# The last 64 rows of a down projection, multiplied in the row halves of TensorE's array, in groups of eight between two output tiles

## The chip, the core and the metric

The kernel runs on one core of one Trainium2 chip. The metric is the device time of one execution in microseconds (us). It was 488.84 us as the median of three runs (487.09, 488.84 and 489.75).

## What is computed

The reference applies a low-rank adapter that is selected for each batch entry, feeds its output through a gated feed-forward block with FP8-quantized activations and weights, and adds the result to the input. Cut to what matters:

```python
x: (8, 256, 1024)                      # 2048 tokens of H = 1024
Bx  = einsum('bni,bri->bnr', x,  B[ids])        # rank 16
c   = einsum('bnr,bor->bno', Bx, A[ids])
gate = q8(c) @ gate_w.T ;  up = q8(c) @ up_w.T  # I = 2752 columns each
hidden = silu(gate) * up
out = x + q8(hidden) @ down_w.T                 # contraction over I = 2752
```

`q8` clips and rounds to FP8 and multiplies the scale back in. The change is in the last product. Its contraction length is 2752 = 21 x 128 + 64, so that one chunk of 64 rows is left over.

## The kernel before

All activations lie transposed, features on the 128 partitions and tokens along the free dimension. The 2048 tokens are cut into four blocks of 512 (`NTB = 4`, `TB = 512`). The contraction and output dimension H is cut into eight tiles of 128 (`NH = 8`), the inner dimension I into 22 chunks (`NI = 22`), of which the last has 64 rows (`TAIL = 64`). TensorE takes 128 x 128 weights, of which `high` picks the upper 16 bits (bf16) out of the 32-bit words that lie in memory, and streams 512 columns of FP8 activations past them.

The program has three stages.

1. *Adapter*, the first 47 us. Products with the small matrices B and A give the FP8 activations `xg`. The products with A (`times_a` at L456, `four_times_a` at L491) have a contraction of only 16; each goes into one of four row groups of the array (partitions 0, 32, 64 and 96 onwards), and the four of a round write four different PSUM tiles `c0` to `c3`. They stand in the middle of full-array products of the next stage: for instance `gate_up(2, 0, between=...)` at L562 puts 32 of them between the gate products and the up products of a block.
2. *Gate and up* (`gate_up`, L503 to L543). For each chunk c of I and each token block t, eight products for the gate and eight for the up values; ScalarE takes the silu (L525) and VectorE multiplies it with the up values into `hid[c]` in FP8 (L526). For the last chunk, gate and up share one set of weights of 64 + 64 columns, so there are eight products. Its gate values come out on PSUM partitions 0 to 63, its up values on 64 to 127, and its result is written to partitions 64 to 127 of `hid[21]`. The partitions 0 to 63 of `hid[21]`, and those of the tail's weight tile `wt`, are set to zero by GpSimd at the start (L393, L394).
3. *Down* (L594 to L623). For each output tile k of 8 and each block t of 4, 22 products run into one PSUM tile `yd`: 21 with the full chunks, and one with `wt` and `hid[21]`, whose upper 64 rows carry the tail and whose lower 64 are the zeros. VectorE scales the sum and adds the residual x (L618), and the result goes out by a DMA on SP's queue (L621).

The order of work on TensorE is the program order of these loops. PSUM is one pool of eight one-bank tiles in rotation (tag `ps`). Weights come through a pool of five 1 MB tiles (`wpool`): each k of Down takes two of them, and their loads (L599) stand in SP's queue together with the output DMAs. ScalarE reads every weight tile and every activation tile once for a check of the values (`note_low_bits` L403, `note_squares` L410). The check's count is read near the end (`outside`, L575), and a general version of the kernel runs instead if the count isn't zero, which with these inputs it is. The tail's weights `wt` come by one DMA (L571), issued at 27.5 us.

Of the kernel before, what the change touches and what calls it, by code (L numbers as in the profile page):

```python
# [8 lines left out]
F32 = mybir.dt.float32  # L9
BF16 = mybir.dt.bfloat16  # L10
FP8 = mybir.dt.float8e4
# [3 lines left out]
ALU = mybir.AluOpType  # L15
AX = mybir.AxisListType

P = 128
T = 2048
# [6 lines left out]
NI = (I + P - 1) // P  # L26
TAIL = I - (NI - 1) * P
TB = 512
NTB = T // TB
# [14 lines left out]
def high(ap):  # L44

    return ap.bitcast(BF16)[..., 1::2]


def low(ap):
    return ap.bitcast(U16)[..., 0::2]  # L50
# [201 lines left out]
def adaln_ffn(  # L252
# [13 lines left out]
    nc = tc.nc  # L266
    const = ctx.enter_context(tc.tile_pool(name="const", bufs=1))
    psum = ctx.enter_context(
        tc.tile_pool(name="psum", bufs=8, space=bass.MemoryType.PSUM)
    )  # L270
# [10 lines left out]
    NSQ = 2 * NTB + NI  # L281
# [5 lines left out]
    with ExitStack() as fast:  # L287
        acts = fast.enter_context(tc.tile_pool(name="acts", bufs=1))
        lora = fast.enter_context(tc.tile_pool(name="lora", bufs=1))
        wpool = fast.enter_context(tc.tile_pool(name="w", bufs=5))  # L290
        work = fast.enter_context(tc.tile_pool(name="work", bufs=3))


        xs = [acts.tile([P, NH, TB], F32, name=f"x{t}") for t in range(NTB)]
        xg = [acts.tile([P, NH, TB], FP8, name=f"xg{t}") for t in range(NTB)]
        hid = [acts.tile([P, T], FP8, name=f"hid{c}") for c in range(NI)]

# [41 lines left out]
        def load_gate_up(c):  # L341
            n = NH if c == NI - 1 else 2 * NH
            w = wpool.tile([P, 2 * NH, P], F32, tag="w", name="w_gu")[:, :n]
            at = c * 2 * NH * P
            nc.sync.dma_start(  # L345
                out=w, in_=w_gu[:, at : at + n * P].rearrange("p (k n) -> p k n", n=P)
            )
            w_of[c] = w
# [30 lines left out]
        down_s = const.tile([P, 1], F32, name="down_s")  # L379
# [10 lines left out]


        wt = acts.tile([P, NH, P], F32, name="w_dt")
        nc.gpsimd.memset(wt[:TAIL], 0.0)  # L393
        nc.gpsimd.memset(hid[NI - 1][:TAIL], 0.0)  # L394

        def junk_like(ap):
            size = prod(ap.shape[1:])
            junk = work.tile([P, 2 * NH * P], BF16, tag="junk", name="junk", bufs=1)
            return shaped(junk[:, :size], ap)

        def note_low_bits(w, rows, column):
            tc.keep_in_program_order(
                nc.scalar.activation(  # L403
                    junk_like(w), low(w), AF.Copy, accum_out=lows[:rows, column : column + 1]
                )
            )

        def note_squares(q, rows, column):
            tc.keep_in_program_order(
                nc.scalar.activation(  # L410
                    junk_like(q), q, AF.Square, accum_out=squares[:rows, column : column + 1]
                )
            )
# [28 lines left out]
        def round_to(to, c, engine):  # L442
            scale = inv[:, GATE_IN : GATE_IN + 1]
            if engine is nc.vector:
                nc.vector.tensor_scalar(to, c, scale, None, ALU.mult, saturate=False)  # L445
            else:
                nc.scalar.activation(to, c, AF.Copy, scale=scale, saturate=False)  # L447
# [37 lines left out]
        def four_times_a(bm, pairs):  # L485
            for i in pairs:
# [11 lines left out]
                for q in range(4):  # L498
                    to = xg[2 + q // 2][:, 2 * i : 2 * i + 2, bass.ts(q % 2, SEQ)]
                    round_to(to, cs[q], nc.vector if q % 2 else nc.scalar)  # L500


        def gate_up(c, t, between=None):  # L503
            tail = c == NI - 1
            w = w_of[c]
            cols = bass.ts(t, TB)
            ys = []
            for j in range(1 if tail else 2):
                y = psum.tile([P, TB], F32, tag="ps", name=f"y{j}")
                order = ORDER if t < 2 else range(NH)  # L510
                for k in order:
                    nc.tensor.matmul(  # L512
                        y,
                        lhsT=high(w[:, j * NH + k, :]),
                        rhs=xg[t][:, k, :],
                        start=(k == order[0]),
                        stop=(k == order[-1]),
                    )
                ys.append(y)
                if between and not j:  # L520
                    between()
            gates, ups = (ys[0], ys[-1]) if not tail else (ys[0][:TAIL], ys[0][TAIL:])
            rows = slice(TAIL, P) if tail else slice(0, P)
            g = work.tile([P, TB], F32, tag="g", name="g")
            nc.scalar.activation(g[rows], gates, AF.Silu, scale=gate_s[: gates.shape[0]])  # L525
            nc.vector.scalar_tensor_tensor(  # L526
                hid[c][rows, cols],
                in0=ups,
                scalar=up_by_down[rows],
                in1=g[rows],  # L530
                op0=ALU.mult,
                op1=ALU.mult,
                saturate=False,
            )
            if c > 1 and t == (NTB - 1 if c == 2 else 1):
                for done in {2: (0, 2), 3: (1, 3)}.get(c, (c,)):
                    note_low_bits(w_of[done], P, done)
                if c <= 1 + 2 * NTB:
                    i, half = divmod(c - 2, 2)
                    ks = slice(half * NH // 2, (half + 1) * NH // 2)  # L540
                    note_squares(xg[i][:, ks, :], P, c - 2)
                for done in (0, 1) if c == 2 else (c - 1,):
                    note_squares(hid[done], P, 2 * NTB + done)  # L543
# [13 lines left out]
        bm = times_b(1, b_pad)  # L557
# [3 lines left out]
        bm = four_times_b()  # L561
# [6 lines left out]
        for c in range(3, NI):  # L568
            load_gate_up(c)
            if c == NI - 2:  # L570
                nc.sync.dma_start(out=wt[TAIL:], in_=w_d_tail)  # L571
            for t in range(NTB):
                gate_up(c, t)

        def outside():  # L575

            nc.vector.tensor_scalar(ok[:, :NLOW], lows, 0.0, None, ALU.is_le)
            nc.vector.tensor_scalar(
                ok[:, NLOW : NLOW + NSQ], squares, SAME_MAX**2, None, ALU.is_lt
            )  # L580
            least = const.tile([P, 1], F32, name="least")
            nc.vector.tensor_reduce(least, ok, AX.X, ALU.min)
            found = const.tile([P, 1], F32, name="found")
            nc.vector.tensor_scalar(found, least, 0.5, None, ALU.is_lt)
            ones = const.tile([P, 1], F32, name="ones")
            nc.vector.memset(ones, 1.0)
            count = psum.tile([P, TB], F32, tag="ps", name="count")
            nc.tensor.matmul(count[:1, :1], lhsT=found, rhs=ones, start=True, stop=True)  # L588
            count_i = const.tile([1, 1], I32, name="count_i")
            nc.vector.tensor_copy(count_i, count[:1, :1])  # L590
            return nc.values_load(count_i[0:1, 0:1], min_val=0, max_val=P)


        for k in range(NH):  # L594
            ws = []
            for half in range(2):
                n = HALF - half
                w = wpool.tile([P, 2 * NH, P], F32, tag="w", name="w_d")[:, :n]
                nc.sync.dma_start(out=w, in_=w_d[k][:, half * HALF : half * HALF + n, :])  # L599
                note_low_bits(w, P, NI + 2 * k + half)  # L600
                ws += [w[:, i, :] for i in range(n)]
            if k == 0:
                note_squares(hid[NI - 1], P, NSQ - 1)
                note_low_bits(wt, P, NLOW - 1)
            for t in range(NTB):
                cols = bass.ts(t, TB)
                y = psum.tile([P, TB], F32, tag="ps", name="yd")
                for c in range(NI):
                    tail = c == NI - 1
                    nc.tensor.matmul(  # L610
                        y,
                        lhsT=high(wt[:, k, :] if tail else ws[c]),
                        rhs=hid[c][:, cols],
                        start=(c == 0),
                        stop=tail,
                    )
                o = work.tile([P, TB], F32, tag="o", name="o")
                nc.vector.scalar_tensor_tensor(  # L618
                    o, in0=y, scalar=down_s, in1=xs[t][:, k, :], op0=ALU.mult, op1=ALU.add
                )  # L620
                nc.sync.dma_start(out=outT[bass.ts(k, P), cols], in_=o)  # L621
                if k == NH - 1 and t == NTB - 2:
                    others = outside()  # L623

    with tc.If(others > 0):
        general(
# [78 lines left out]
```

## Time and profile before

| | |
|---|---|
| median of three runs | 488.84 us (487.09 to 489.75) |
| the profiled execution | 486.88 us, of which the profile's span is 485.1 us |
| granted TensorE clock | 0.996 |
| TensorE (PE) busy | 476.7 us, 98% of the span |
| VectorE (DVE) busy | 105.1 us, 22% |
| ScalarE (ACT) busy | 192.0 us, 40% |
| GpSimd (POOL) busy | 2.9 us, 1% |
| gate and up products (L512) | 298.2 us busy in 1376 |
| down products, full chunks (L610 with `w_d`) | 150.3 us busy in 672 |
| down products, tail (L610 with `w_dt`) | 12.1 us busy in 32 |
| DMA | 52.39 MB, mean 108 GB/s |

Matmuls are pipelined, so the duration of one (379 ns) overlaps that of the next. The distance from one start to the next is what a product costs in a row of them. A line of the timeline gives the start in us, the length in us, the engine, the source line, the operation with its tiles and shapes, and how many instructions are merged in it. In brackets stands the engine's idle time before it, with what ended it. PEld is the loading of weights, which overlaps PE. `SPq` is SP's queue, which issues DMAs.

### The profile page before, as it was taken

The numbers are of one execution on the slowest core, as the hardware profiler recorded it, in microseconds if no ns is written. First come the engines' busy times: TensorE is split into PE (matmuls) and PEld (weight loads), VectorE is DVE, ScalarE is ACT, GpSimd is POOL, SyncE is SP. The second block draws the span as 40 slices with busy tenths as digits, with TensorE's granted clock in tenths as the row PEclk, the third lists the DMA queues.
The fourth block names the chain that finished last, engine by engine and source line by source line (L and its number), as shares of the span: only waits on it lengthen the run. The fifth ranks groups of instructions, "written<-read, shape, count | busy, mean of one in ns | idle before, by whom it ended". The sixth has DMA issues, their size and how long they took to land.

```text
span 485.1 us, 5786 instructions
## 1 busy us (share of the span) xinstructions
PE 476.7 (98%) x2416; PEld 224.2 (46%) x2416; DVE 105.1 (22%) x159; ACT 192.0 (40%) x243; POOL 2.9 (1%) x6
## 2 busy tenths in 40 slices
PE   8999999999999999999999999999999999999995
PEld 8445444444444444444444444444444444444442
DVE  1435221212121212121212121222111111112111
ACT  1234239955556654534354545459102112011000
POOL 2000000000000000000000000000000000000000
PEclk9999999999999999999999999999999999999998
DMA  8996004422221112222221011113514515423111
GB/s 297 331 388 245 1 0 176 172 86 88 86 88 56 42 77 88 86 86 88 86 65 36 31 59 55 61 55 104 157 69 154 168 62 171 120 103 120 43 67 50
DMA packets 13092, 52.39 MB, mean 108 GB/s; under 512 B 1538, under 2 KB 2562, under 8 KB 9474
## 3 DMA queue, kind: packets, MB, share of 16 engines
q1 hardware_dynamic: 12768, 51.80, 30.9%
q8 instruction: 21, 0.34, 0.3%
q10 hardware_dynamic: 290, 0.14, 0.1%
q14 instruction: 13, 0.11, 0.1%
HBM read 43.55 MB, written 8.39 MB: 107 GB/s over the span
## 4 chain that ended last, share of the span: by engine, by line
PE 91%; DMA 6%; SPq 2%; issue 0%; DVE 0%
PE y L512 58%; PE yd L610 31%; DMA w_gu<-w_gu 5%; PE c L491 1%; SPq L337 1%; SPq L319 0%; SPq L312 0%; DMA ids_i<-ids 0%; SPq L317 0%; DVE o L618 0%; SPq L345 0%; SPq L331 0%; PE count L588 0%
## 5 line engine op out<-in xcount | busy, mean ns | idle before, releaser
L512 PE MATMUL y<-xg,w_gu 128*128 128x512 fp8e4 x1376 | 298.2, 379 | 0.8 <-ACT xg L447 0.5
L512 PEld LDWEIGHTS <-w_gu 128*128 128x128 bf16 x1376 | 134.2, 98 | 164.1 <-issue 2.2
L610 PE MATMUL yd<-hid,w_d 128*128 128x512 fp8e4 x672 | 150.3, 379 | 0.0
L525 ACT ACTIVATE g<-y,gate_s 128x512 f32<-128x512 f32 (+1 forms) x88 | 60.0, 683 | 146.8 <-PE y L512 146.7
L526 DVE SCALAR_TENSOR_TENSOR hid<-y,up_by_down,g 128x512 fp8e4<-128x512 f32 (+1 forms) x88 | 66.0, 751 | 225.7 <-PE y L512 158.3
L610 PEld LDWEIGHTS <-w_d 128*128 128x128 bf16 x672 | 65.7, 98 | 79.1
L403 ACT ACTIVATE junk<-w_d 128x1408 bf16<-128x1408 uint16 (+1 forms) x16 | 21.2, 1324 | 89.2 <-DMA w_d<-w_d 89.1
L618 DVE SCALAR_TENSOR_TENSOR o<-yd,down_s,x 128x512 f32<-128x512 f32 x32 | 24.0, 750 | 122.0 <-PE yd L610 122.0
L410 ACT ACTIVATE junk<-hid 128x2048 bf16<-128x2048 fp8e4 x22 | 41.9, 1906 | 0.5
L403 ACT ACTIVATE junk<-w_gu 128x2048 bf16<-128x2048 uint16 (+1 forms) x22 | 41.0, 1865 | 0.1
L410 ACT ACTIVATE junk<-xg 128x2048 bf16<-128x2048 fp8e4 x8 | 15.3, 1906 | 0.2
L447 ACT ACTIVATE xg<-c,inv 128x512 fp8e4<-128x512 f32 x16 | 9.7, 688 | 13.8 <-PE c L456 12.1
L445 DVE TENSOR_SCALAR xg<-c,inv 128x512 fp8e4<-128x512 f32 x16 | 10.9, 744 | 6.8 <-PE c L456 3.8
L610 PE MATMUL yd<-hid,w_dt 128*128 128x512 fp8e4 x32 | 12.1, 379 | 0.0
L550 PE MATMUL warm<-zeros 128*128 128x128 bf16 x78 | 7.4, 287 | 1.0 <-DVE zeros L277 1.0
L431 PE MATMUL bx<-x,b_pad 128*64 128x256 f32 x64 | 7.7, 382 | 0.3 <-DVE b_pad L420 0.3
L550 PEld LDWEIGHTS <-zeros 128*128 128x128 bf16 x78 | 7.2, 136 | 1.0 <-DVE zeros L277 1.0
L431 PEld LDWEIGHTS bx<-x,b_pad 128*64 128x64 f32 x64 | 5.5, 137 | 2.1 <-DVE b_pad L420 0.5
L610 PEld LDWEIGHTS <-w_dt 128*128 128x128 bf16 x32 | 3.1, 98 | 3.8
L456 PE MATMUL c<-bm,a_sel 16*128 16x256 f32 x64 | 4.0, 387 | 0.5 <-DVE bm L439 0.5
L403 ACT ACTIVATION_READ_ACCUMULATOR junk<-w_gu 128x1 f32 x22 | 4.2, 192 | 0.0
L410 ACT ACTIVATION_READ_ACCUMULATOR junk<-hid 128x1 f32 x22 | 4.1, 188 | 0.0
(37 smaller groups left out, 31.5 us busy)
## 6 DMA issues: line engine op xcount, KB each, us to landing
w_gu<-w_gu SPq DMA_DIRECT2D x21, 1024.0 KB, 4.9
outT<-o SPq DMA_DIRECT2D x32, 256.0 KB, 2.1
x<-x SPq DMA_DIRECT2D x7, 1024.0 KB, 8.9
w_d<-w_d SPq DMA_DIRECT2D x8, 704.0 KB, 5.0
w_d<-w_d SPq DMA_DIRECT2D x8, 640.0 KB, 3.8
x<-x SPq DMA_DIRECT2D x2, 512.0 KB, 5.8
a_sel<-a SPq DMA_DIRECT2D x4, 128.0 KB, 5.5
w_gu<-w_gu SPq DMA_DIRECT2D x1, 512.0 KB
```

Source lines behind the costliest of these rows:

```text
L337: nc.sync.dma_start(out=xs[t][:, ks, :], in_=x4[t][:, ks, :])
L403: nc.scalar.activation(junk_like(w), low(w), AF.Copy, accum_out=lows[:rows, column : column + 1])
L410: nc.scalar.activation(junk_like(q), q, AF.Square, accum_out=squares[:rows, column : column + 1])
L431: nc.tensor.matmul(bx[64 * j : 64 * (j + 1)], lhsT=b_pad[:, j, k].rearrange("p o r -> p (o r)"), rhs=xs[t][:, k, bass.ts(j, SEQ)], start=( ...
L445: nc.vector.tensor_scalar(to, c, scale, None, ALU.mult, saturate=False)
L447: nc.scalar.activation(to, c, AF.Copy, scale=scale, saturate=False)
L512: nc.tensor.matmul(y, lhsT=high(w[:, j * NH + k, :]), rhs=xg[t][:, k, :], start=(k == order[0]), stop=(k == order[-1]),)
L525: nc.scalar.activation(g[rows], gates, AF.Silu, scale=gate_s[: gates.shape[0]])
L526: nc.vector.scalar_tensor_tensor(hid[c][rows, cols], in0=ups, scalar=up_by_down[rows], in1=g[rows], op0=ALU.mult, op1=ALU.mult, saturate=F ...
L550: nc.tensor.matmul(warm[:, :P], lhsT=zeros, rhs=zeros, start=(i == 0), stop=(i == 77))
L610: nc.tensor.matmul(y, lhsT=high(wt[:, k, :] if tail else ws[c]), rhs=hid[c][:, cols], start=(c == 0), stop=tail,)
L618: nc.vector.scalar_tensor_tensor(o, in0=y, scalar=down_s, in1=xs[t][:, k, :], op0=ALU.mult, op1=ALU.add)
```

## The change

- The tail's hidden values get a tile of their own, `hid_tail`, of bf16 with 128 partitions, 2 and 512. Odd blocks lie on partitions 0 to 63, even blocks on partitions 64 to 127 (`half_of`), two blocks along the free dimension. VectorE first writes the FP8 values into a small tile `tail`, and then copies them to `hid_tail` as bf16.
- The tail's weights are loaded twice, into both partition halves of `wt`. The zeros, and GpSimd's two memsets that wrote them, are gone.
- In Down the tail's products have 64 rows, and two blocks lie in the two row halves of the array (`tail_of`). They are grouped: after the 4 x 21 full products of an even k come the four tail products of this k, and at once the four tail products of k + 1, which open the PSUM tiles of k + 1. Then follow the 4 x 21 full products of k + 1, of which the last closes each tile.
- For an even k the four evictions (`finish`) come together behind its tail group. For an odd k each follows its block, as before.
- `note_squares` for the tail reads `hid_tail`, 1024 elements of a partition instead of 2048.

```diff
-        hid = [acts.tile([P, T], FP8, name=f"hid{c}") for c in range(NI)]
+        hid = [acts.tile([P, T], FP8, name=f"hid{c}") for c in range(NI - 1)]
+        hid_tail = acts.tile([P, 2, TB], BF16, name="hid_tail")
...
-        nc.gpsimd.memset(wt[:TAIL], 0.0)
-        nc.gpsimd.memset(hid[NI - 1][:TAIL], 0.0)
...
+        def half_of(t):
+            return slice(0, TAIL) if t % 2 else slice(TAIL, P)
...
+            if tail:
+                to = lora.tile([P, 2 * TB], FP8, tag="bm", name="tail", bufs=2)[half_of(t), :TB]
+            else:
+                to = hid[c][:, cols]
...
             nc.vector.scalar_tensor_tensor(
-                hid[c][rows, cols],
+                to,
...
+            if tail:
+                nc.vector.tensor_copy(hid_tail[half_of(t), t // 2], to)
...
-                nc.sync.dma_start(out=wt[TAIL:], in_=w_d_tail)
+                for t in range(2):
+                    nc.sync.dma_start(out=wt[half_of(t)], in_=w_d_tail)
...
+        def tail_of(k, ys, start):
+            for t in range(NTB):
+                nc.tensor.matmul(
+                    ys[t],
+                    lhsT=high(wt[half_of(t), k, :]),
+                    rhs=hid_tail[half_of(t), t // 2],
+                    start=start,
+                    stop=not start,
+                )
+
+        def finish(k, t, y):
+            o = work.tile([P, TB], F32, tag="o", name="o")
+            nc.vector.scalar_tensor_tensor(
+                o, in0=y, scalar=down_s, in1=xs[t][:, k, :], op0=ALU.mult, op1=ALU.add
+            )
+            nc.sync.dma_start(out=outT[bass.ts(k, P), bass.ts(t, TB)], in_=o)
...
-                note_squares(hid[NI - 1], P, NSQ - 1)
+                note_squares(hid_tail, P, NSQ - 1)
...
+            first = k % 2 == 0
+            if first:
+                ys = [psum.tile([P, TB], F32, tag="ps", name=f"yd{t}") for t in range(NTB)]
             for t in range(NTB):
-                cols = bass.ts(t, TB)
-                y = psum.tile([P, TB], F32, tag="ps", name="yd")
-                for c in range(NI):
-                    tail = c == NI - 1
+                for c in range(NI - 1):
                     nc.tensor.matmul(
-                        y,
-                        lhsT=high(wt[:, k, :] if tail else ws[c]),
-                        rhs=hid[c][:, cols],
-                        start=(c == 0),
-                        stop=tail,
+                        ys[t],
+                        lhsT=high(ws[c]),
+                        rhs=hid[c][:, bass.ts(t, TB)],
+                        start=(first and c == 0),
+                        stop=(not first and c == NI - 2),
                     )
...
+                if not first:
+                    finish(k, t, ys[t])
                 if k == NH - 1 and t == NTB - 2:
                     others = outside()
+            if first:
+                tail_of(k, ys, start=False)
+                for t in range(NTB):
+                    finish(k, t, ys[t])
+                ys = [psum.tile([P, TB], F32, tag="ps", name=f"yd{t}") for t in range(NTB)]
+                tail_of(k + 1, ys, start=True)
```

More of the change, by code (lines that the diff above doesn't have):

```diff
@@ L602, in adaln_ffn @@
             if k == 0:
-                note_squares(hid[NI - 1], P, NSQ - 1)
+                note_squares(hid_tail, P, NSQ - 1)
                 note_low_bits(wt, P, NLOW - 1)
+            first = k % 2 == 0
+            if first:
+                ys = [psum.tile([P, TB], F32, tag="ps", name=f"yd{t}") for t in range(NTB)]
             for t in range(NTB):
-                cols = bass.ts(t, TB)
-                y = psum.tile([P, TB], F32, tag="ps", name="yd")
-                for c in range(NI):
-                    tail = c == NI - 1
+                for c in range(NI - 1):
                     nc.tensor.matmul(
-                        y,
-                        lhsT=high(wt[:, k, :] if tail else ws[c]),
-                        rhs=hid[c][:, cols],
-                        start=(c == 0),
-                        stop=tail,
-                    )
[L617 to L621, printed above, removed]
+                        ys[t],
[3 more added lines that the diff above has]
+                        stop=(not first and c == NI - 2),
+                    )
+                if not first:
+                    finish(k, t, ys[t])
                 if k == NH - 1 and t == NTB - 2:
                     others = outside()
+            if first:
[4 more added lines that the diff above has]
+                tail_of(k + 1, ys, start=True)
     with tc.If(others > 0):
```

## The prediction

> **What bounds the kernel now.** I read the page's first part (busy time), then the chain that ended last, then the groups by line, and last the timeline in narrow windows around the places where TensorE's array already changes its shape.
>
> ```profile
> PE 476.7 (98%) x2416; PEld 224.2 (46%) x2416; DVE 105.1 (22%) x159; ACT 192.0 (40%) x243; POOL 2.9 (1%) x6
> ...
> PE 91%; DMA 6%; SPq 2%; issue 0%; DVE 0%
> ...
> L610 PE MATMUL yd<-hid,w_d 128*128 128x512 fp8e4 x672 | 150.3, 379 | 0.0
> L610 PE MATMUL yd<-hid,w_dt 128*128 128x512 fp8e4 x32 | 12.1, 379 | 0.0
> ```
>
> TensorE is 91% of the chain, the early transfers are nearly all the rest, and before Down's products it stands idle for 0.0 us. So whatever shortens TensorE's row of products in Down shortens the end by as much, unless a new wait appears. The tail products take as long as full ones (379 ns each). What one costs is the distance of starts:
>
> ```profile
> 327.09 147.20 PE yd L610 x682
> 474.29 0.12 PE count L588 x2
> 474.41 4.87 PE yd L610 x22
> 479.30 0.75 DVE o L618
> ```
>
> 147.20 / 682 gives 0.216 us a product, tail ones among them. All 32 tail products cost 32 x 0.216 = 6.9 us, half of it for rows of zeros.
>
> The trace of before holds no product in a row half, but it holds near relatives: the adapter's products, in row quarters, standing between full products.
>
> ```profile
> 39.55 1.90 PE L512 MATMUL y<-xg,w_gu 128*128 128x512 fp8e4 x8 [0.17 <-DMA w_gu<-w_gu]
> 41.38 2.01 PE L491 MATMUL c<-bm,a_four 16*128 16x256 f32 x32
> 43.32 1.90 PE L512 MATMUL y<-xg,w_gu 128*128 128x512 fp8e4 x8
> ...
> 41.38 0.71 PE L491 MATMUL c<-bm,a_four 16*128 16x256 f32 x8
> ...
> 42.35 1.04 PE L491 MATMUL c<-bm,a_four 16*128 16x256 f32 x16
> ```
>
> The last line: 16 products, four rounds of four, in 1.04 us. Without the last one's own 0.374 us that is 0.666 us for three rounds, 0.216 us a round with 0.007 us between the four of a round. Four row groups at once take the pitch of one full product. The first three lines: from full product to full product again, 43.32 - 39.55 = 3.77 us pass for eight full products and eight rounds, which at 0.216 us are 3.45 us. So one excursion costs 0.32 us over its rounds. It splits so: going in, 41.38 - 39.55 - 8 x 0.216 = 0.10 us; within, the first two rounds take 0.71 - 0.374 - 0.02 = 0.32 us instead of 0.216, 0.10 us for the first weights, which nothing hides; going out the rest, some 0.12 us. The excursion at 23.21 to 26.98 us is also 3.77 us long.
>
> [...] Here too a row group's next weights load beside its own product, or the pitch would not be 0.216 us. [...] The trace: 98 ns for bf16, 184 ns for fp32.
>
> **The change part by part.**
>
> *Removed:* 32 full tail products, eight to each pair of k: 8 x 0.216 = 1.73 us a pair, on the path.
>
> *Added:* for each pair one excursion with four rounds of two, 4 x 0.216 = 0.86 us, and 0.007 us for the second half. Its overhead, between bounds:
> - going in and out, 0.09 us each by the relatives (0.10 and 0.12 less what first weights cost);
> - the first weights, in and out: 0.01 us each if bf16 weights behave as they do on the way out before (three full products from 43.32 us take 0.82 us, three amid a row take 0.81), 0.10 us if as the fp32 ones.
>
> The sum is 0.21 to 0.30 us. I take 0.23, nearer the lower end, since the new weights are bf16. An excursion then costs 0.86 + 0.01 + 0.23 = 1.10 us and saves 0.63 us; four of them save **2.5 us** (2.2 to 2.6 between the bounds). Beyond these, nothing shows 64-row tiles with bf16: at best the changes cost nothing and 4 x 0.86 = 3.4 us go; at worst each round shows its weights load (98 ns), which takes back 4 x 4 x 0.1 = 1.6 us and leaves 0.9.
>
> *Moved: evictions of even k.* Four come together, 4 x 0.75 = 3.0 us on VectorE, where each stood 4.74 us from the next. There are three output buffers, so the fourth waits for the first's output DMA: about 0.75 + 0.34 + 2.1 = 3.2 us after the first began, instead of 2.25. Behind it on VectorE is the eviction of k + 1's first block, due after 21 x 0.216 = 4.5 us more of products. Nobody on TensorE waits: k + 1's tiles are the other four banks, which the previous odd k left, and the banks of k come back with k + 2, 18 us later. Cost nothing; that cover gone, about 1 us a pair.
>
> *SP's queue.* In the changed order of instructions seven outputs stand together between the weight loads of k + 3's halves. A load waits for the tile that its k's predecessor two and a half k earlier gives up, at the end of a k; the outputs ahead of it end by then, within some 4 us, and the tile is needed at least one k (18 us) later, with 3.8 to 5.0 us for its transfer. Nothing.
>
> *Gate and up's last chunk.* Four copies on VectorE, not in the trace of before; the nearest row is the 425 ns copy of 128x256, and I take 0.4 us. A block has 8 x 0.216 = 1.73 us of products, VectorE then has 0.75 + 0.4 us to do. The first tail product stands 84 full products (18 us) behind. Nothing.
>
> *The second load of the tail's weights,* 256 KB: issued behind the three weight loads of 25.95 us, the first landed 18.7 us later. The one load that TensorE waits for (0.17 us at 39.55) is ahead of it in the same queue. Nothing; were the transfers mixed, at most 256 KB at the page's 388 GB/s, 0.7 us.
>
> *GpSimd's memsets* (2.7 us at the start) and half of ScalarE's 1.9 us square are off the path. The end, product, eviction, output, is as before.
>
> The profiled execution took 486.88 us, 1.8 of it outside the span; it would become 484.4. The shown median is 488.84, 2.0 above that execution, so I forecast 488.84 - 2.5 = **486.3 us**.
>
> **The rivals.**
> 1. *Overlap, but weights in the open.* If row halves' loads can't go beside their products, 0.9 us is saved: 487.9. Against it: the row quarters hide loads of 184 ns.
> 2. *The halves don't run together* (the change doesn't do what it says): eight products one after another, as before, and four overheads of 0.23: 0.9 us slower, 489.7. Against it: four quarters do run together. For it: the quarters are 16 rows of fp32, 256 columns, never 64 of bf16 and 512.
> 3. *Slower: each step between the halves counts as a change of mode.* [...] 32 x 0.09 + 0.9 = 3.8 us, 492.6. It decides as soon as a tail product costs more than (1.73 - 0.23) / 8 = 0.19 us on average. Against it: 0.007 us between quarters.
> 4. *Cheaper changes:* [...] 3.2 us saved, 485.6.
>
> **How the numbers follow.** Forecast 60%, rival 1 14%, rival 2 9%, rival 3 7%, rival 4 8%, 2% for what I don't see. A measurement of this kernel tells 0.5%, 2.4 us, from no change, and the forecast lies just past that: of its 60% I count 36 as faster, 23 as the same and 1 as slower, its runs spreading by about 1.4 us. With rival 4 and little of rival 1, faster is 0.45; rival 1 and most of rival 2 bring the same to 0.41; the rest, 0.14, is slower. The range reaches from 484.2 (rival 4 in a quick run) to 489.5 (rivals 1 and nearly 2) and leaves out rival 3.
>
> **What would show it.** In the changed profile: tail products in pairs 0.007 us apart, rounds 0.216 us apart, each group some 1.1 us from the last full product's end of pitch to the next full one; TensorE busy less by 2 to 3 us; four evictions back to back with no idle TensorE behind; waits before Down's full products still near 0.0. Wrong would be: tail products 0.2 us or more apart one by one, idle time before the first full product of an odd k, or a weight load landing late.

## The result, and the profile after

The changed kernel took 485.81 us (median of six runs, 484.40 to 486.74) against 489.14 us for the kernel before (six runs, 487.09 to 489.75). The ratio is 0.9939 with a 95% interval of 0.9912 to 0.9966: faster by 0.3 to 0.9%, or 1.7 to 4.3 us. The medians lie 3.3 us apart. The forecast was 486.3 us and 2.5 us of gain.

Two profiled executions can be compared far more sharply than the medians, if one looks at Down alone. In the chain that ended last (start, length, what), Down of the changed kernel reads:

```profile
327.07 18.13 PE yd L640 x84
345.20 0.97 PE yd L608 x8
346.17 36.37 PE yd L640 x168
382.53 0.97 PE yd L608 x8
...
472.00 4.66 PE yd L640 x21
476.66 0.02 issue
476.68 0.75 DVE o L618
```

From the first piece of Down to the last eviction pass 476.68 - 327.07 = 149.61 us. In the kernel before it was 479.30 - 327.09 = 152.21. Down is 2.60 us shorter. In these two executions it starts at the same time, so that the span, too, fell by 2.6, from 485.1 to 482.5 us. That they start together is chance: a second profile of the changed kernel begins Down at 328.28 us, and the eleven traces of this case at 327.07 to 329.46. This spread is as large as the gain and arises before Down. The length of Down, in contrast, came out at 149.61 and 149.62 us in the two profiles of the changed kernel. So it is the length of Down that the experiments compare.

One group, in the timeline:

```profile
343.74 1.46 PE L640 MATMUL yd<-hid,w_d 128*128 128x512 fp8e4 x6
345.13 1.04 PE L608 MATMUL yd<-hid_tail,w_dt 64*128 64x512 bf16 x8
346.10 4.28 PE L640 MATMUL yd<-hid,w_d 128*128 128x512 fp8e4 x19
```

Eight products of 64 rows stand between the starts 345.13 and 346.10, 0.97 us apart. One by one at 0.216 us they would have taken 1.73. The line merges the eight. The trace's record of each start shows four pairs, 3 to 4 ns from one product to the other of a pair and 0.216 us from pair to pair (0.227 after the first). Below, such a pair of products side by side is a round, and the array's way from its full shape into the row halves and back is an excursion.

The groups of the page (busy us and mean ns of one behind the bar, then idle time before them):

```profile
L640 PE MATMUL yd<-hid,w_d 128*128 128x512 fp8e4 x672 | 146.1, 379 | 0.0
L608 PE MATMUL yd<-hid_tail,w_dt 64*128 64x512 bf16 x32 | 4.2, 379 | 0.0
L640 PEld LDWEIGHTS <-w_d 128*128 128x128 bf16 x672 | 65.4, 98 | 79.8 <-issue 1.7
```

A tail product still lasts 379 ns, but 32 of them cover only 4.2 us where the old ones covered 12.1 (each overlaps its neighbours in either case). No product is recorded as waiting for a bank or a transfer: the idle time before both rows is 0.0. (The changes of shape don't show as idle time: the starts on either side of one lie about 0.31 us apart, and the recorded 379 ns of a product cover that.) The 1.7 us of "issue" at the weight loads are the four returns to the full array, 0.42 us each. The first weights after these four returns are not loaded early: in each group their load begins 4 ns before its product (in the first at 346.095 us), where the next one begins 0.215 us before its own.

### The profile page after: what moved, and what is told of

Its sections match the earlier page's. It is cut to its first block, busy times and chain, and to the rows that moved or that the text cites. A ratio compares the mean times of both kernels' runs of the same rounds, so it can differ in the third digit from the quotient of the medians.

```text
span 482.5 us, 5789 instructions
## 1 busy us (share of the span) xinstructions
PE 473.2 (98%) x2416; PEld 221.1 (46%) x2416; DVE 105.9 (22%) x163; ACT 191.1 (40%) x243; POOL 0.2 (0%) x4
## 4 chain that ended last, share of the span: by engine, by line
PE 96%; DMA 1%; ACT 1%; DVE 0%; ACTq 0%; issue 0%
PE y L516 62%; PE yd L640 30%; PE bx L432 2%; DMA b_sel<-b 1%; PE c L492 1%; PE yd L608 1%; PE bx L475 1%; PE c L457 1%; ACT xg L448 0%; ACT L275 0%; DVE o L618 0%; ACTq L315 0%; ACTq L274 0%; DVE bm L440 0%; DVE b_pad L421 0%
## 5 line engine op out<-in xcount | busy, mean ns | idle before, releaser
L640 PE MATMUL yd<-hid,w_d 128*128 128x512 fp8e4 x672 | 146.1, 379 | 0.0
L534 DVE SCALAR_TENSOR_TENSOR hid<-y,up_by_down,g 128x512 fp8e4<-128x512 f32 x84 | 63.1, 751 | 220.0 <-PE y L516 158.3
L618 DVE SCALAR_TENSOR_TENSOR o<-yd,down_s,x 128x512 f32<-128x512 f32 x32 | 23.0, 748 | 118.3 <-PE yd L608 62.6
L411 ACT ACTIVATE junk<-hid 128x2048 bf16<-128x2048 fp8e4 x21 | 40.0, 1905 | 0.4
L608 PE MATMUL yd<-hid_tail,w_dt 64*128 64x512 bf16 x32 | 4.2, 379 | 0.0
L492 PE MATMUL c<-bm,a_four 16*128 16x256 f32 x64 | 4.1, 389 | 0.0
L534 DVE SCALAR_TENSOR_TENSOR tail<-y,up_by_down,g 64x512 fp8e4<-64x512 f32 x4 | 3.0, 756 | 4.9 <-ACT g L533 4.8
## 6 DMA issues: line engine op xcount, KB each, us to landing
w_dt<-w_d_tail SPq DMA_DIRECT2D x2, 256.0 KB, 18.5
```

Source lines behind the costliest of these rows:

```text
L411: nc.scalar.activation(junk_like(q), q, AF.Square, accum_out=squares[:rows, column : column + 1])
L534: nc.vector.scalar_tensor_tensor(to, in0=ups, scalar=up_by_down[rows], in1=g[rows], op0=ALU.mult, op1=ALU.mult, saturate=False,)
L608: nc.tensor.matmul(ys[t], lhsT=high(wt[half_of(t), k, :]), rhs=hid_tail[half_of(t), t // 2], start=start, stop=not start,)
L618: nc.vector.scalar_tensor_tensor(o, in0=y, scalar=down_s, in1=xs[t][:, k, :], op0=ALU.mult, op1=ALU.add)
L640: nc.tensor.matmul(ys[t], lhsT=high(ws[c]), rhs=hid[c][:, bass.ts(t, TB)], start=(first and c == 0), stop=(not first and c == NI - 2),)
```

## The experiments

All times of Down below are read as above, from the first piece of Down in the chain to the last eviction's start, in one profiled execution. The ratio is that of the timed runs to the kernel before.

| kernel | Down, us | against the changed kernel | ratio to before, 95% interval |
|---|---|---|---|
| before | 152.21 | +2.60 | |
| changed | 149.61 | | 0.9939 (0.9912 to 0.9966) |
| changed, again | 149.62 | +0.01 | 0.9941 (0.9925 to 0.9958) |
| each_k | 150.48 | +0.87 | 0.9963 (0.9949 to 0.9978) |
| each_pair | 152.09 | +2.48 | 1.0002 (0.9991 to 1.0012) |
| grouped_full | 152.22 | +2.61 | 0.9999 (0.9989 to 1.0008) |
| one_half | 153.06 | +3.45 | 1.0021 (1.0012 to 1.0030) |
| ahead | 150.36 | +0.75 | 0.9962 (0.9947 to 0.9977) |
| mid | 149.62 | +0.01 | 0.9954 (0.9938 to 0.9971) |
| two_and_two | 149.63 | +0.02 | 0.9957 (0.9942 to 0.9972) |
| four_and_four | 149.66 | +0.05 | 0.9940 (0.9924 to 0.9957) |

The intervals of the last three overlap that of the changed kernel. What their ratios differ by isn't in Down: in mid, for instance, Down begins 2.4 us later than in the changed kernel's first profile and is as long.

**The changed kernel, repeated** beside ahead, mid and two_and_two.

> The changed kernel once more, beside the three that follow. All theories: 0.994 of before.

It gave 485.64 us against 488.62. The gain is there a second time, with a narrower interval, and Down is as long as in the first profile to 0.01 us.

**Is it the overlap? grouped_full** keeps all of the change but the halves:

```diff
-                    lhsT=high(wt[half_of(t), k, :]),
-                    rhs=hid_tail[half_of(t), t // 2],
+                    lhsT=high(wt[:, k, :]),
+                    rhs=hid_tail[:, t // 2],
```

> The changed kernel in its order of work, evictions, copies and transfers, but each tail product takes all 128 rows of the weights and of the tail's values, so that a block's output holds the tail of both blocks of its pair. My theory, the gain is the overlap of the halves alone: 32 x 0.216 = 6.9 us for the tail products, ratio 1.000 to before, and no change of mode in the trace. Rival, the gain comes from what else was changed (memsets gone, order, the start of the kernel): as the changed kernel, 0.994.

Its chain opens and closes Down with these lines:

```profile
327.82 18.13 PE yd L640 x84
480.04 0.75 DVE o L618
```

Down took 152.22 us, that of the kernel before to 0.01, and the timed runs agree to 0.1% (0.9989 to 1.0008). So the memsets that are gone, the copies, the second load of weights, the grouping and the moved evictions together are worth nothing that can be seen, in either direction. (Four of the 32 tail products are missing from this trace's records; the length of Down doesn't depend on them.)

**Is a product of 64 rows shorter in itself? one_half** keeps the 64 rows but puts all of them into one half:

```diff
-                    lhsT=high(wt[half_of(t), k, :]),
-                    rhs=hid_tail[half_of(t), t // 2],
+                    lhsT=high(wt[TAIL:, k, :]),
+                    rhs=hid_tail[TAIL:, t // 2],
```

> The changed kernel, but all eight tail products of a group in the upper row half, so that odd blocks take the tail of the even block of their pair. Nothing can run side by side. My theory: 4 x (8 x 0.216 + 0.21) = 7.8 us for the tail products, 0.9 us slower than before (ratio about 1.002), 3.5 over the changed kernel. Rival, a product of 64 rows is itself shorter: between the changed kernel and before.

The timeline of its first group:

```profile
344.31 1.89 PE L640 MATMUL yd<-hid,w_d 128*128 128x512 fp8e4 x8
346.13 1.90 PE L608 MATMUL yd<-hid_tail,w_dt 64*128 64x512 bf16 x8
347.96 1.25 PE L640 MATMUL yd<-hid,w_d 128*128 128x512 fp8e4 x5
```

Its eight tail products last 1.90 us, exactly as long as eight full products with a first weights load among them (1.90 us for `y` in the trace of before), instead of 1.04. By the record of their starts they follow each other every 0.216 us (0.228 after the first). Here a product of 64 rows takes the 0.216 us of a full one; half the rows save nothing. The kernel is 3.45 us slower than the changed one and 0.85 slower than before, which is the price of four excursions with nothing gained in them. With grouped_full, this shows that the gain is the running side by side, and nothing else.

**What does a change of mode cost? each_k and each_pair** make more and shorter excursions. (A change of mode is one between the array's full shape and its halves.) The group of a k stands behind its first block, that of a pair of blocks behind the pair's first; the tail closes this block and opens the others.

```diff
-        def tail_of(k, ys, start):
-            for t in range(NTB):
+        def tail_of(k, ys, ts, closed=()):
+            for t in ts:
...
-                    start=start,
-                    stop=not start,
+                    start=t not in closed,
+                    stop=t in closed,
...
-                if not first:
-                    finish(k, t, ys[t])
+                if t == 0:                                   # each_k
+                    tail_of(k, ys, range(NTB), (0,))
+                finish(k, t, ys[t])
...
+                if t % 2 == 0:                               # each_pair
+                    tail_of(k, ys, (t, t + 1), (t,))
+                finish(k, t, ys[t])
```

> One change of mode in and out for each k (eight excursions of four tail products) instead of one for two k. The group of a k stands behind its first block. My theory, an excursion costs its rounds and 0.21 us: 8 x (2 x 0.216 + 0.21) = 5.2 us for all tail products, 0.9 us more than the changed kernel and 1.7 less than before; ratio to before about 0.9965. Rival, the changes of mode cost nothing and the gain is all overlap: as the changed kernel.

> An excursion for every pair of blocks, 16 of two tail products. My theory: 16 x (0.216 + 0.21) = 6.9 us, the whole gain is given back, as before within 0.2 us (ratio 1.000), 2.6 us over the changed kernel. Rival, the changes of mode cost nothing: as the changed kernel, ratio 0.994.

Pieces of the chains, each_k first:

```profile
327.14 4.53 PE yd L638 x21
331.68 0.54 PE yd L608 x4
332.21 18.24 PE yd L638 x84
```

```profile
327.95 4.53 PE yd L638 x21
332.49 0.32 PE yd L608 x2
332.81 9.17 PE yd L638 x42
```

Groups of eight, four and two products take 0.97, 0.54 and 0.32 us in the chain: 0.22 us less for each round of two that is left out. Over the whole of Down, an excursion's cost over its rounds follows from what it saves against full products:

- changed, 4 excursions: 2.60 / 4 = 0.65 saved of 8 x 0.216 = 1.73, so 1.08 spent, of which four rounds are 0.86: 0.21 us over;
- each_k, 8 excursions: 1.73 / 8 = 0.22 saved of 0.86, so 0.65 spent, two rounds are 0.43: 0.22 us over;
- each_pair, 16 excursions: 0.12 / 16 = 0.01 saved of 0.43, so 0.42 spent, one round is 0.22: 0.21 us over.

Three sizes give one constant. The kernels also differ in where the groups stand and when tiles are evicted; mid, below, shows for the group of eight that this costs nothing where the banks are free. An excursion of a single pair just breaks even, as the timed runs say too (1.0002). The rival, that the changes are free, falls.

**Does it matter where the group stands? ahead and mid.** In ahead the group of eight stands wholly in front of an even k, the first one excepted; in mid it stands behind the first block of an even k. In both every block is evicted right behind itself.

```diff
+            if k % 2 == 0:
+                both = [
+                    [psum.tile([P, TB], F32, tag="ps", name=f"yd{t}") for t in range(NTB)]
+                    for i in range(2)
+                ]
+                if k:                                        # ahead
+                    for i in range(2):
+                        tail_of(k + i, both[i], range(NTB))
+            ys = both[k % 2]
...
+                if k % 2 == 0 and t == 0:                    # mid
+                    tail_of(k, both[0], range(NTB), (0,))
+                    tail_of(k + 1, both[1], range(NTB))
+                finish(k, t, ys[t])
```

> The group of eight stands wholly ahead of an even k and opens all eight tiles (for the first two k behind the first block, since the tail's values come late there). Each block is evicted behind itself. My theory: the eighth product needs the bank of the last block of the k before, whose eviction starts 0.42 us behind the start of its last product and takes 0.75 us, so it starts at about 1.25 us behind that instead of 0.97: 0.3 us of wait in three groups, 0.8 us over the changed kernel. Rival, banks come back in time: as the changed kernel.

> The group of eight stands behind the first block of an even k, closes this block and opens the other seven. The four evictions no longer come together, so none waits for an output's transfer. My theory, the late fourth eviction costs nothing now: as the changed kernel within 0.1 us in the trace. Rival, the backlog of evictions costs something: faster than the changed kernel.

The timeline of ahead in front of k = 2:

```profile
365.36 1.28 PE L608 MATMUL yd<-hid_tail,w_dt 64*128 64x512 bf16 x8
365.46 0.75 DVE L618 SCALAR_TENSOR_TENSOR o<-yd,down_s,x 128x512 f32<-128x512 f32 x1 [3.78 <-PE yd L646]
...
366.57 1.69 PE L646 MATMUL yd<-hid,w_d 128*128 128x512 fp8e4 x7
```

The eight products last 1.28 us instead of 1.04. The eviction of the block before runs from 365.46 to 366.21 us, and the eighth product needs its bank: with the 0.38 us of one product taken off, the group's end puts its start at about 366.26 us, 0.05 us behind that eviction. By the record of the starts it is the eighth alone that is late: it begins 0.25 us behind the seventh, instead of 3 to 4 ns. That is 0.25 us in each of three groups, and 0.75 us in Down: the cover that the prediction named for the changed kernel's place, other banks that had been left long before, is real, and these 0.25 us a group are what it costs to lose it.

In mid, Down is the changed kernel's to 0.01 us. Its waits show no eviction that waits for an output's transfer; all 32 wait for a product:

```profile
DVE o L618 <- PE yd L643: 108.7, 28, 4.5
DVE o L618 <- PE yd L608: 10.5, 4, 4.1
```

In the changed kernel there are four that wait for a transfer:

```profile
DVE o L618 <- PE yd L608: 62.6, 4, 17.7
DVE o L618 <- PE yd L640: 42.8, 13, 4.0
DVE o L618 <- DMA outT<-o: 13.0, 4, 4.7
```

(Total us, times, longest.) So these 13 us of VectorE's time cost nothing.

**In which order do products start? two_and_two and four_and_four** change the order of blocks in a group: in the first, two of the upper half and then two of the lower for each k; in the second, four of the upper half and then four of the lower for both k.

```diff
-            for t in range(NTB):
+            for t in (0, 2, 1, 3):                           # two_and_two
...
+            for i, t in [(i, t + h) for h in range(2) for i in range(2) for t in (0, 2)]:
+                nc.tensor.matmul(                            # four_and_four
+                    both[i][t],
+                    lhsT=high(wt[half_of(t), k + i, :]),
+                    rhs=hid_tail[half_of(t), t // 2],
+                    start=(i == 1),
+                    stop=(i == 0),
+                )
```

> The changed kernel with the tail products of a k in the order of blocks 0, 2, 1, 3: two of the upper half, then two of the lower. My theory, products start strictly in order and a half takes one at a time: a group then needs five steps of 0.216 us instead of four, 4 x 0.216 = 0.9 us over the changed kernel (ratio to before 0.996). Rival, the queue lets a product of the free half go ahead: as the changed kernel.

> The changed kernel, with the group's products in the order: four of the upper half (blocks 0 and 2 of both k), then four of the lower. What the two-and-two order left open: whether a product of the free half goes ahead of those that wait for the busy one. If it does, over a distance of three: pairs 0.22 us apart as in the changed kernel, 0.66 us from first to last start, ratio 0.994. If products start strictly in order: the lower half begins with the last upper one, seven steps, 1.5 us from first to last, 4 x 0.65 = 2.6 us more than the changed kernel, as before (1.000). In between: the queue looks ahead by fewer.

My theory fell. The first groups, two_and_two and then four_and_four:

```profile
346.17 1.04 PE L608 MATMUL yd<-hid_tail,w_dt 64*128 64x512 bf16 x8
```

```profile
345.74 1.05 PE L608 MATMUL yd<-hid_tail,w_dt 64*128 64x512 bf16 x8
```

Both last as long as the changed kernel's 1.04 us, to 0.01 us, that is four rounds. In one_half a half took one product per 0.216 us. At that pace and in strict order the group of four_and_four would have needed six steps after its first start, about 1.68 us with the last product's own 0.38 (the expectation counted seven; its 2.6 us rest on six); its 1.05 us are three. So in these groups a product of the free half went ahead of up to three that stand before it.

Another explanation would be that the products were put into another order before they reached the chip. The records of the starts speak against it, since they also keep which product waits for VectorE, which writes the tail's values. In the changed kernel all four tail products of the first k wait for it, each for its own block. In two_and_two and four_and_four the wait is missing at one of the four. That fits block 1 in the order written there, since its product follows that of block 2, which has waited for a later copy already. Yet the product without this wait starts second, 6 ns behind the first in two_and_two and 14 ns in four_and_four, where it is the fifth of the program. By these records the order of the program was as written, and the order of starts was not. By which rule a product is let past, and over how many at most, no run here shows.

No version beat the changed kernel. Whether the tail's values could stay FP8 in the halves, which would spare the four copies, wasn't tried; grouped_full shows no cost of the copies and the rest together.

## Why the prediction was right

- *What bounds the kernel.* TensorE's row of products did carry its gain to the end of Down unshortened, 2.60 us. The medians lie 3.3 us apart, 0.7 us more than that. The interval of 1.7 to 4.3 us holds both, and the difference isn't in Down.
- *Removed and added.* The 0.63 us saved per group came out at 0.65. The overhead, taken as 0.24 us (0.23, and 0.01 for the second half), was 0.21. The starts in the first group of the changed kernel show its parts: going in 0.096 us over the pitch of a product, going out 0.093, the first weights 0.011 and 0.010, and the step to the second half 0.003. The excursions of the adapter in the trace of before had told each to 0.01 us: 0.09 for either change and, for bf16 weights, 0.01. (As listed, the prediction's parts add up to 0.20 at the low end, where it has 0.21.) The part of the quarters' 0.32 us that went to fp32 weights was rightly left out. The 0.02 us that the prediction added above the low end, in case the new weights load in the open, weren't needed.
- *Rivals 1 to 3* each needed the halves to hide less than the quarters do. Rival 1, weights in the open, would have spaced the rounds by 0.3 us (0.216 and a load's 0.098), and they are 0.216 apart. Rival 3, a change of mode at each step between halves, would have put 0.09 us there, and the step is 3 to 4 ns. Rival 2's price was computed as 0.9 us over before, and one_half, which is that rival made real, gave 0.85. Rival 4, cheaper changes with 3.2 us saved, is excluded by the 2.60 us in Down and the constant 0.21.
- *The moved evictions:* free, as forecast, but their size was off. The fourth was to begin 3.2 us behind the first; in the first group it began 6.7 us behind it. VectorE's timeline of the changed kernel, and SP's queue:

```profile
345.55 2.07 DVE L618 SCALAR_TENSOR_TENSOR o<-yd,down_s,x 128x512 f32<-128x512 f32 x3 [12.45 <-PE yd L608]
352.29 1.41 DVE L618 SCALAR_TENSOR_TENSOR o<-yd,down_s,x 128x512 f32<-128x512 f32 x2 [4.66 <-DMA outT<-o]
...
343.11 2.48 SPq L629 DMA_DIRECT2D w_d<-w_d  x2
346.33 14.69 SPq L621 DMA_DIRECT2D outT<-o  x7
```

The term that was mis-sized is the output's landing, taken as the median of 2.1 us. The first output of this group was issued right behind the two weight loads that the end of the even k released, and landed 5.8 us after its issue. The trace of before already holds outputs that stand right behind such a pair of loads. Five of them have a recorded landing, and it comes 4.6 to 5.1 us after the issue, which the median hides. The spread of the landings (least, median, most), before and after:

```profile
DMA to landing us min/median/max: 2.1/2.1/5.1
DMA to landing us min/median/max: 2.1/2.2/5.8
```

The next block's eviction was held up by it as well. There was enough cover all the same: those banks come back 18 us later. The seven outputs had left SP's queue at 361.0 us, ahead of the next weight load, which was no later than before (362.31 us, 362.77 before).
- *Copies, second weights load, memsets:* the copies took 0.42 us each (0.4 assumed), and the first of the two loads, the one with a recorded landing, landed 18.5 us after issue (18.7 before). That Down's start was 327.1 us in both traces proves nothing, given its spread; grouped_full, which has all of these and takes as long as the kernel before, does.
- *The uncertain part,* beside the rivals, was whether 2.5 us would stand clear of the runs' spread. The gain came out at 0.6%. That nothing changed is excluded, the interval's upper end being 0.9966; whether the gain is above 0.5% the timed runs don't tell.

## What to carry to other kernels

In this kernel products of 64 rows gained nothing by being short (0.216 us one by one, as full ones). They gained by running in pairs (0.216 us a pair), and each excursion into row halves had the same price for two, four and eight products, 0.21 to 0.22 us, about one product of 512 columns. So collect as many as the PSUM banks allow before changing the mode: here two products broke even (Down 152.09 us against 152.21), and eight, one for each bank, saved 0.65 us. Put the group where its banks were left long ago (a bank that was still being evicted cost 0.25 us a group), and look for the price in whatever part of the kernel already changes the array's shape.

## What the runs showed of the hardware that was not expected

- A tail product could pass products of the other half that stood before it in the program: the group took 1.04 to 1.05 us in three different orders, where one_half's took 1.90, and in four_and_four the fifth product of the program started second, 14 ns behind the first. A strict order would have cost 0.9 us and 2.6 us by the expectations; Down grew by 0.02 and 0.05 us.
- An output of 256 KB issued behind two weight loads landed after up to 5.8 us where the median was 2.2. It was not expected, though the trace of before had it, with up to 5.1 us.
